# Gathers released in blocks of four buffers, and smaller blocks in the streamed table, in a graph-layer kernel

## The chip, the cores and the metric

The kernel runs on one core of one Trainium2 chip. The metric is the device time of one execution in microseconds. Three timed executions of the kernel before took 1646.1 to 1649.81 us, with a median of 1647.18 us. The profile is one further execution.

## The reference

There are 12,500 nodes with 128 features each, and 200,000 edges that are sorted by their target `dst`. The targets are drawn so that low node numbers have very many edges and high ones few. Every edge has one of four types, and every type has a 128x128 matrix and a bias.

```python
h = jnp.maximum(_layernorm(x, axis=-1), 0.0)
xs = h[src]
for i in range(4):
    msgs = msgs + jnp.where((edge_type == i)[:, None], xs @ W[i] + b[i], 0.0)
out = x + segment_sum(msgs, dst, num_segments=12500)
```

## The kernel before, in words

The edges are cut into 1563 chunks of 128. **Setup** (until about 193 us): `x` is read in spans of three rows a partition (`load_span`, L472), normalized, split into three bf16 parts that add up to the f32 value, and written to a table `htab` in DRAM, 768 bytes a node. The spans lie in the buffers of the pool `rows` (`hpool`, L234), which the gathers take over later. The edges of the first 528 chunks are brought into "slots" (`make_slots`, L797), and the 48 chunks after them are worked from rows of `x` (`add_up_raw`, L610).

**The main part** weaves two independent kinds of work on TensorE.

*Dense work*, for the first 528 chunks, goes in 19 batches. `count` (L938) multiplies one-hot matrices `o` that VectorE makes (L957, L965) into counts of edges for each node, type and source (`pt`, L983), which ScalarE casts to bytes (L989). `multiply` (L1021) then multiplies the whole table by these counts: for each of the 98 blocks `j` of the table, three matmuls with the table as the weights (`pa`, L1033). The table is streamed from DRAM once a batch: SyncE's queue issues one load `hs` (L1029) for `HB` = 6 blocks (L59), 17 loads a batch, into a ring of `STREAM` = 4 buffers (L62). A load waits until TensorE has read the buffer that it fills. Other transfers stand in the same queue in between: the edge lists of later chunks (L210), the finished rows of the output (`out_dram`, L698) and the rows of `x` that are added to the next ones (`xo`, L677).

*Sparse work*, for the other 987 chunks, goes in groups of 16 (60 groups, then 12, 8, 4 and 3). `gather` (L538) is called for the group after the one being worked on. It takes one buffer of `rows` for each two chunks (`HG` = 2) and issues one indirect DMA a chunk from GpSimd's queue: 128 rows of 768 bytes, picked by `srcT`. There are 11 buffers. A gather that fills a buffer waits for the last matmul that reads what lay in it. `sum_up` (L569) multiplies each chunk's rows by a one-hot matrix `oh` (L561), three matmuls a chunk (`ps`, L578); after every four chunks ScalarE copies the sums out (L581). `weigh` (L586) multiplies by the type matrices (`py`, L605), and VectorE adds the result into a ring of output rows (`ring`, L666).

The order on TensorE, VectorE and ScalarE in the main part is written out by the program (`manual_schedule`, L1302): the loop at L1304 takes the steps of `sum_up` for a group, and after each step as many steps of the dense work as `pace` (L1079) says, by columns of matmul. GpSimd's and SyncE's instructions stand in the order that the framework's scheduler gives them. `held_by` (L517) adds a wait to an instruction by hand.

After about 1591 us the dense work is over, and the last groups and output rows follow.

Of the kernel before, what the change touches and what calls it, by code (L numbers as in the profile page):

```python
# [55 lines left out]
C0 = 528  # L56
UB = 27
MANY = 16
HB = 6  # L59
SLOTS = 4  # L60
SETS = 4
STREAM = 4  # L62
# [3 lines left out]
HG = 2  # L66
# [2 lines left out]
SOON = (RAW * 16) + HG  # L69

TURN = 4


@with_exitstack
def kernel(
# [10 lines left out]
    nc = tc.nc  # L86
# [35 lines left out]
    def window_of(c):  # L122

        m = min((c - C0) // G, FULL)
        end = (C0 + (m + 1) * G if m < FULL else T) * P / E
        a_node = E * ((end**2 + 1 / N) ** 0.5 - end)
        return next((n for n in range(8, WIN, 2) if (n - 1) * a_node > P + 5 * P**0.5), WIN)
# [14 lines left out]
    left = threes + len(two)  # L142
# [3 lines left out]
    for i, n in enumerate(sizes_of):  # L146
# [4 lines left out]
        of = alone[3 * many_at : 3 * (many_at + n1)]  # L151
# [69 lines left out]

    srcT = const.tile([P, TURN, P], I32, name="srcT")
    keyT = const.tile([P, TURN, P], F32, name="keyT")
    brow = const.tile([1, BR * BC], I32, name="brow")
# [6 lines left out]
    flag = const.tile([P, 1], I32, name="flag")  # L231

    mid = ExitStack()
    hpool = mid.enter_context(tc.tile_pool(name="rows", bufs=11))  # L234
    opool = mid.enter_context(tc.tile_pool(name="onehots", bufs=2))
    spool = mid.enter_context(tc.tile_pool(name="typed", bufs=2))
    x_ps = mid.enter_context(tc.tile_pool(name="x_ps", bufs=4, space=PSUM))
# [30 lines left out]
    def prep_edges(m0, m1, prep, QB):  # L268
# [16 lines left out]
        for q in range(n):  # L285
            nc.tensor.transpose(pg[:, q, :], sf[:, q, :], ident)
        nc.scalar.copy(srcT[:, m0 % TURN : m0 % TURN + n, :], pg[:, :n, :])
        nc.vector.tensor_copy(head[:, m0:m1], di[:, :n, 0])
# [9 lines left out]
        for q in range(n):  # L298
            nc.tensor.transpose(pk[:, q, :], key[:, q, :], ident)
        nc.scalar.copy(keyT[:, m0 % TURN : m0 % TURN + n, :], pk[:, :n, :])  # L300
        nc.vector.tensor_reduce(ends[:, m0:m1, 0], rel[:, :n], AX.X, ALU.max)
# [4 lines left out]
    def prep_steps(m, prep):  # L306
# [26 lines left out]
        nc.tensor.transpose(pg[:, 1, :], key[:, 0, :], ident)  # L333
        nc.scalar.copy(srcT[:, m % TURN, :], pg[:, 0, :])
        nc.scalar.copy(keyT[:, m % TURN, :], pg[:, 1, :])

# [180 lines left out]
    def held_by(one, by, reason):  # L517
        tc.add_manual_dep(
            one.ins,
            by.name,  # L520
            mybir.DependencyInfo(mybir.DependencyClass.Sync, mybir.DependencyReason.DATA),
            reason=reason,
        )

    def gather_raw(k, by):
# [9 lines left out]
                held_by(one, by, "rows of x come while the table is made, spread over its blocks")  # L535
        return hm

    def gather(t0, g):  # L538
        got = []
        for h0 in range(0, g, HG):  # L540
            hm = hpool.tile([P, HG * D3], BF16, name="hm")
            for i in range(h0, min(h0 + HG, g)):
                at = (t0 + i) % (TURN * P)
                one = nc.gpsimd.indirect_dma_start(  # L544
                    out=hm[:, (i - h0) * D3 : (i - h0 + 1) * D3],
                    out_offset=None,
                    in_=htab,
                    in_offset=bass.IndirectOffsetOnAxis(ap=srcf[:, at : at + 1], axis=0),
                )
                if i == h0 and gates and t0 + i >= SOON:  # L550
                    held_by(one, gates.pop(0), "the first rows come while the slots are made, not ahead of them")
            got.append(hm)
        return lambda i, c: got[i // HG][:, (i % HG * 3 + c) * D : (i % HG * 3 + c + 1) * D]

    def one_hots_of(t0, g):
        K = NT * window_of(C0 + t0)
        oh = opool.tile([P, G, KM], BF16, name="oh")[:, :, :K]

        def make(i):
            at = (t0 + i) % (TURN * P)  # L560
            nc.vector.tensor_scalar(oh[:, i, :], iota_b[:, :K], keyf[:, at : at + 1], None, ALU.is_equal)  # L561

        return oh, [lambda i=i: make(i) for i in range(g)]
# [5 lines left out]
    def sum_up(t0, g, rows, oh, last):  # L569
        win = window_of(C0 + t0)  # L570
        K = NT * win
        sb = spool.tile([P, G * KM], F32, name="sb")[:, : G * K].rearrange("p (g t n) -> p g t n", g=G, t=NT)
        for i0 in range(0, g, SG):
            i1 = min(i0 + SG, g)
            ps = s_ps.tile([P, 512], F32, name="ps")[:, : SG * K].rearrange("p (i n) -> p i n", i=SG)
            for i in range(i0, i1):
                for c in range(3):
                    nc.tensor.matmul(ps[:, i - i0, :], rows(i, c), oh[:, i, :], start=(c == 0), stop=(c == 2))  # L578
                if i % HG and i + 1 < i1:
                    yield (i + 1) / g  # L580
            nc.scalar.copy(sb[:, i0:i1].rearrange("p g t n -> p g (t n)"), ps[:, : i1 - i0, :])  # L581
            yield i1 / g

        finish.append(weigh(t0, g, oh, sb, last))

    def weigh(t0, g, oh, sb, last):  # L586
        win = window_of(C0 + t0)

        def bank():
            to = x_ps.tile([P, G * WIN], F32, name="pt") if last else y_ps.tile([P, G * WIN], F32, name="py")  # L590
            return to[:, : G * win].rearrange("p (g n) -> p g n", g=G)

        ohv = oh.rearrange("p g (t n) -> p g t n", t=NT)
        pc = bank()
        for t in range(NT):
            nc.tensor.matmul(  # L596
                pc[t * CG : (t + 1) * CG, :g, :], three, ohv[:, :g, t, :], start=True, stop=True, tile_position=(0, t * CG)
            )
        cnt = spool.tile([P, G * WIN], BF16, name="cnt")[:, : G * win].rearrange("p (g n) -> p g n", g=G)
        nc.scalar.copy(cnt[:, :g], pc[:, :g])  # L600
        yield True
        py = bank()
        nc.tensor.matmul(py[:, :g, :], b128, cnt[:, :g, :], start=True, stop=False)
        for t in range(NT):
            nc.tensor.matmul(py[:, :g, :], wsb[:, t, :], sb[:, :g, t, :], start=False, stop=(t == NT - 1))  # L605
        adds.extend(ring_adds(t0, g, lambda i: py[:, i, :], win))
        yield True
# [413 lines left out]
    def multiply(vs, counts):  # L1021
# [3 lines left out]
        pa = a_ps.tile([P, 512], F32, name="pa")  # L1025
        for j0 in range(0, NW, HB):
            j1 = min(j0 + HB, NW)
            hs = hsp.tile([P, HB, D3], BF16, name="hs")
            nc.sync.dma_start(hs[:, : j1 - j0, :], htab.rearrange("(p j) f -> p j f", j=NW)[:, j0:j1, :])  # L1029
# [265 lines left out]
    leaving = []  # L1295
    soon = []
    rows = gather(RAW * G, G)
    oh, made = one_hots_of(RAW * G, G)
    for m in made:
# [4 lines left out]
    for gi, (t0, g) in list(enumerate(zip(starts, sizes)))[RAW:]:  # L1304
# [12 lines left out]
        if gi < final:  # L1317
            rows = gather(starts[gi + 1], sizes[gi + 1])
        parts = -(-g // HG)
        when = min(2, parts - 1)  # L1320
        todo = len(side) + G + 1 + (G if finish else 0)
        for j, part in enumerate(sum_up(t0, g, *now, gi >= FULL)):
            late, tails[:] = list(tails), []
            while work and spent < pace(gi, part):
                spent = next(work, None)
                if spent is None:
                    work = None
            for f in late:
                f()
            if checks and next(checks[0], None) is None:  # L1330
                checks.pop(0)
            if j == 0:
                if finish:
                    next(finish[0])
                if gi < final:
                    oh, made = one_hots_of(starts[gi + 1], sizes[gi + 1])
                    side += made
            if j == when:
                if finish:
                    next(finish.pop(0))  # L1340
                side.append(lambda: [ending.pop(0)() for _ in list(ending)])
                side += adds
                adds.clear()
                todo = min(todo, len(side) * parts // max(1, parts - 1 - j))
            left = todo * (parts - 1 - j) // parts - (0 if j >= when else todo - len(side))
            while side and len(side) > left:
                side.pop(0)()
            for _ in range(2):
                if leaving:
                    leaving.pop(0)()  # L1350
# [171 lines left out]
```

## Time and profile before

| | us |
|---|---|
| median of three executions | 1647.18 |
| lowest, highest | 1646.1, 1649.81 |
| the profiled execution's own time | 1651.06 |
| its span, first to last instruction | 1649.2 |
| TensorE's mean granted clock | 0.957 of full speed |
| dense and sparse work together on TensorE | 193 to 1591 |

A group of instructions is named by source line, engine and operation, with the tiles written and read (`pa<-counts,hs`), its count, its busy time, the mean of one in ns, and the engine's idle time just before them with what ended it. "issue" is idle time that ended by nothing that the profile shows; "remote" a wait whose releaser is not told. PEld is the load of weights into TensorE, and a q behind an engine's name stands for its queue of instructions (SPq issues DMAs). The chain of waits follows the work that ended last back to the start.

### The profile page before, as it was taken

The page shows a single profiled execution, that of the slowest core. Times are in us where ns is not written, and L with a number is a line of the kernel's source. Part 1 is how long each engine was busy: PE and PEld are TensorE (multiplying, and loading weights), DVE is VectorE, ACT ScalarE, POOL GpSimd, SP SyncE. Part 2 cuts the span into 40 slices and gives each one's busy share as a digit, 9 for nine tenths or more (in the row PEclk, how much of TensorE's full clock was granted, in tenths as well). Part 3 has the DMA queues.
Part 4 walks back from the last instruction along what each step waited for, and adds up shares of the span by engine and source line. Part 5 has one row for each costly group of instructions (what it writes and reads, how often), then busy time and mean ns, then how long its engine had stood idle before and what let it go on. Part 6 is the DMA issues. An engine that isn't in the chain of part 4 may idle for free.

```text
span 1649.2 us, 33169 instructions
## 1 busy us (share of the span) xinstructions
PE 1457.4 (88%) x11293; PEld 958.5 (58%) x11293; DVE 1041.5 (63%) x5387; ACT 458.7 (28%) x1121; POOL 1011.6 (61%) x1062
## 2 busy tenths in 40 slices
PE   5678789999899999999999999999999999998975
PEld 2236476666566566666666666656565656565654
DVE  8792977666585766657576666657564756574333
ACT  6494222222222222222222222222222222222011
POOL 7435566666666666666666666666666566666562
PEclk9785799999999999999999999999999999999997
DMA  7452377766667766666666667666666566666652
GB/s 221 129 212 75 107 220 220 217 197 213 200 206 211 217 194 212 197 208 208 207 202 201 200 209 220 181 210 203 180 219 198 175 194 211 184 189 193 210 169 70
DMA packets 138411, 317.02 MB, mean 192 GB/s; under 512 B 25880, under 2 KB 78666, under 8 KB 138235
## 3 DMA queue, kind: packets, MB, share of 16 engines
q1 hardware_dynamic: 89323, 214.61, 41.7%
q0 software_dynamic: 48912, 100.24, 20.8%
q8 instruction: 89, 1.46, 0.4%
q14 instruction: 87, 0.71, 0.1%
HBM read 298.71 MB, written 16.04 MB: 191 GB/s over the span
## 4 chain that ended last, share of the span: by engine, by line
PE 81%; issue 8%; DVE 8%; ACT 2%; DMA 1%; DVEq 0%; SPq 0%; POOL 0%; ACTq 0%
PE pa L1033 47%; PE pt L983 12%; PE py L605 7%; PE ps L578 7%; DVE o L957 1%; PE pt L1047 1%; PE ps L635 1%; PE py L596 1%; PE pt L691 1%; DVE oh L561 1%; DVE o L965 1%; DVE ring L666 1%; PE pt L857 1%; DVE stt L440 1%; PE pt L854 0%
## 5 line engine op out<-in xcount | busy, mean ns | idle before, releaser
L544 POOL DMA_INDIRECT hm<-htab,srcT x987 | 954.7, 967 | 575.6 <-issue 226.0
L1033 PE MATMUL pa<-counts,hs 128*128 128x324 fp8e4 (+1 forms) x5586 | 1000.5, 304 | 50.2 <-issue 47.1
L1033 PEld LDWEIGHTS <-hs 128*128 128x128 bf16 x5586 | 519.0, 96 | 325.1 <-issue 84.7
L957 DVE TENSOR_SCALAR o<-iota_n,hkT 128x392 bf16<-128x392 f16 x1211 | 401.2, 331 | 75.4 <-PE pt L983 30.6
L983 PE MATMUL pt<-o,o 128*128 128x396 bf16 x1211 | 378.4, 336 | 37.0 <-DVE o L965 20.0
L989 ACT CAST counts<-pt 128x396 int32<-128x396 f32 x506 | 242.1, 493 | 500.5 <-PE pt L983 172.1
L561 DVE TENSOR_SCALAR oh<-iota_b,keyT 128x56 bf16<-128x56 bf16 (+8 forms) x987 | 167.7, 261 | 265.6 <-PE ps L578 94.6
L581 ACT COPY sb<-ps 128x224 f32<-128x224 f32 (+8 forms) x247 | 98.4, 399 | 480.3 <-PE pt L983 165.0
L578 PE MATMUL ps<-oh,hm 128*128 128x56 bf16 (+8 forms) x2961 | 189.1, 198 | 38.0 <-issue 35.3
L578 PEld LDWEIGHTS <-hm 128*128 128x128 bf16 x2961 | 163.0, 99 | 96.5 <-issue 49.1
L666 DVE TENSOR_TENSOR ring<-ring,py 128x14 f32 (+7 forms) x960 | 167.7, 175 | 65.0 <-PE pa L1033 13.0
L965 DVE TENSOR_SCALAR o<-iota,loT 128x128 bf16<-128x128 bf16 x660 | 178.4, 270 | 0.0
L983 PEld LDWEIGHTS <-o 128*128 128x128 bf16 x1211 | 114.8, 97 | 96.2 <-DVE o L965 27.4
L965 DVE TENSOR_SCALAR o<-iota,loT,byT 128x128 bf16<-128x128 bf16 x461 | 155.4, 337 | 0.0
L605 PE MATMUL py<-sb,wsb 128*128 128x224 f32 (+7 forms) x480 | 129.5, 412 | 1.3 <-issue 1.0
L605 PEld LDWEIGHTS py<-sb,wsb 128*128 128x128 f32 x480 | 88.2, 196 | 27.6 <-issue 5.6
L997 DVE COPY bi<-counts 128x27 int32<-128x27 int32 (+1 forms) x19 | 4.2, 220 | 113.3 <-issue 64.7
L528 POOL DMA_INDIRECT hx<-in_x_dram,srcT x48 | 51.3, 1069 | 35.9 <-DVE stt L440 22.4
L600 ACT CAST cnt<-py 128x224 bf16<-128x224 f32 (+7 forms) x60 | 23.7, 396 | 93.3 <-PE ps L578 29.9
L461 ACT ACTIVATE h<-hm,nmrt,rstdt 128x128 f32<-128x128 f32 x98 | 43.0, 493 | 1.0 <-DVE mvt L444 0.5
L1047 PE MATMUL pt<-sd,wsb 128*128 128x81 f32 (+1 forms) x152 | 25.8, 325 | 4.6 <-issue 4.6
L490 PE MATMUL ps<-h,ident 128*128 128x384 f32 (+1 forms) x34 | 16.3, 563 | 12.7 <-issue 11.6
(235 smaller groups left out, 666.6 us busy)
## 6 DMA issues: line engine op xcount, KB each, us to landing
hs<-htab SPq DMA_DIRECT2D x304, 576.0 KB
hm<-htab,srcT POOLq DMA_INDIRECT x987
htab<-h SPq DMA_DIRECT2D x32, 288.0 KB
xo<-in_x_dram SPq DMA_DIRECT2D x24, 256.0 KB
out_dram<-xo SPq DMA_DIRECT2D x24, 256.0 KB
hs<-htab SPq DMA_DIRECT2D x19, 192.0 KB
hm<-in_x_dram SPq DMA_DIRECT2D x18, 192.0 KB
hm<-in_x_dram SPq DMA_DIRECT2D x14, 168.0 KB
```

Source lines behind the costliest of these rows:

```text
L528: one = nc.gpsimd.indirect_dma_start(out=hm[:, i * D : (i + 1) * D], out_offset=None, in_=x, in_offset=bass.IndirectOffsetOnAxis(ap=srcf[: ...
L544: one = nc.gpsimd.indirect_dma_start(out=hm[:, (i - h0) * D3 : (i - h0 + 1) * D3], out_offset=None, in_=htab, in_offset=bass.IndirectOffse ...
L561: nc.vector.tensor_scalar(oh[:, i, :], iota_b[:, :K], keyf[:, at : at + 1], None, ALU.is_equal)
L578: nc.tensor.matmul(ps[:, i - i0, :], rows(i, c), oh[:, i, :], start=(c == 0), stop=(c == 2))
L581: nc.scalar.copy(sb[:, i0:i1].rearrange("p g t n -> p g (t n)"), ps[:, : i1 - i0, :])
L605: nc.tensor.matmul(py[:, :g, :], wsb[:, t, :], sb[:, :g, t, :], start=False, stop=(t == NT - 1))
L666: nc.vector.tensor_tensor(to, to, of(i), ALU.add)
L957: one = nc.vector.tensor_scalar(o2[:, k, :NB], iota_n, hkT[:, s : s + 1], None, ALU.is_equal)
L965: one = nc.vector.tensor_scalar(o1[:, k], iota_1, loT[:, s : s + 1], by, ALU.is_equal, ALU.mult)
L983: one = nc.tensor.matmul(pb, o1, o2, start=first, stop=last)
L989: nc.scalar.copy(counts[:, :, i * NT : (i + 1) * NT], pb.rearrange("p (b t) -> p b t", t=NT))
L1033: nc.tensor.matmul(pa[:, : 3 * nu * NT].rearrange("p (m v) -> p m v", m=3), hs[:, j - j0, c * D : (c + 1) * D], of, start=(j == 0 and c == 0),
```

## The change

Three things are changed. The ring of row buffers has 12 instead of 11 places. A load of the streamed table carries 5 blocks instead of 6, so there are 20 loads a batch (19 of five blocks and one of three), and the four buffers of the ring hold 20 blocks instead of 24. And gathers are put into blocks of up to eight chunks, that is four buffers, counted from the start of each group: every gather of a block is made to wait for the matmul that reads the last of the four buffers' earlier contents. `taken` counts buffers, `read` lists the last reading matmul of each buffer in order, and `left` is the number of the reader to wait for; where that matmul is not yet written out when the gather is, `waiting` keeps the gather until it is.

```diff
-HB = 6
+HB = 5
...
+ROWS = 12
+BLOCK = 8
...
-    hpool = mid.enter_context(tc.tile_pool(name="rows", bufs=11))
+    hpool = mid.enter_context(tc.tile_pool(name="rows", bufs=ROWS))
...
+    taken = [0]
+    read = []
+    waiting = {}
...
         for h0 in range(0, g, HG):
+            taken[0] += 1
+            left = taken[0] + (min(h0 // BLOCK * BLOCK + BLOCK, g) - h0 - 1) // HG - 1 - ROWS
             hm = hpool.tile([P, HG * D3], BF16, name="hm")
...
+                if left >= 0:
+                    if left < len(read):
+                        held_by(one, read[left], "a block of rows comes when all of its buffers are free")
+                    else:
+                        waiting.setdefault(left, []).append(one)
...
-                    nc.tensor.matmul(ps[:, i - i0, :], rows(i, c), oh[:, i, :], start=(c == 0), stop=(c == 2))
+                    one = nc.tensor.matmul(ps[:, i - i0, :], rows(i, c), oh[:, i, :], start=(c == 0), stop=(c == 2))
+                if i % HG == HG - 1 or i == g - 1:
+                    for later_one in waiting.pop(len(read), []):
+                        held_by(later_one, one.ins, "a block of rows comes when all of its buffers are free")
+                    read.append(one.ins)
```

## The prediction

> **What bounds the kernel now.** I read the page first: the busy shares, the slices, the chain of waits and the costliest groups.
>
> ```profile
> span 1649.2 us, 33169 instructions
> PE 1457.4 (88%) x11293; PEld 958.5 (58%) x11293; DVE 1041.5 (63%) x5387; ACT 458.7 (28%) x1121; POOL 1011.6 (61%) x1062
> ...
> PE   5678789999899999999999999999999999998975
> ...
> PE 81%; issue 8%; DVE 8%; ACT 2%; DMA 1%; DVEq 0%; SPq 0%; POOL 0%; ACTq 0%
> ...
> L544 POOL DMA_INDIRECT hm<-htab,srcT x987 | 954.7, 967 | 575.6 <-issue 226.0
> L1033 PE MATMUL pa<-counts,hs 128*128 128x324 fp8e4 (+1 forms) x5586 | 1000.5, 304 | 50.2 <-issue 47.1
> ...
> L578 PE MATMUL ps<-oh,hm 128*128 128x56 bf16 (+8 forms) x2961 | 189.1, 198 | 38.0 <-issue 35.3
> ```
>
> TensorE is busy 88% of the span, and it makes 81% of the chain; transfers make 1% of it and GpSimd nothing. The change touches only transfers and the waits ahead of them, so I then asked for the main part alone, in a view by stretches (length, busy time and count of each engine, granted clock, share of the DMA engines, GB/s):
>
> ```profile
> 193.00:1591.00 1398.00, 1290.28 (x10479) 860.47 (x10477) 877.23 (x4608) 336.36 (x805) 888.43 (x918) 0.99 0.66 202
> ```
>
> Here TensorE is busy 1290.3 of 1398.0 us, 92%. All its idle time is 108 us, and that is the most that any better supply could give back. The question is who ends it. Next I grouped the instructions by shape, for the readers of the two kinds of transfer:
>
> ```profile
> L1033 PEld LDWEIGHTS <-hs 128*128 128x128 bf16 x5586 | 519.0, 96 | 325.1 <-issue 84.7
> L578 PEld LDWEIGHTS <-hm 128*128 128x128 bf16 x2961 | 163.0, 99 | 96.5 <-issue 49.1 <-DMA hm<-htab,srcT 3.7
> L983 PEld LDWEIGHTS <-o 128*128 128x128 bf16 x1211 | 114.8, 97 | 96.2 <-DVE o L965 27.4 <-issue 24.1
> ```
>
> Gathers ended 3.7 us of waits in the whole run. No wait is put down to the streamed table; hidden waits for it would stand under "issue". But idle time of that name stands before every kind of matmul: 49.1 us at L578 and 24.1 us at L983, which don't read the stream. So I take it as TensorE's own, and the kernel as bound by TensorE's work.
>
> **Part 1, gathers in blocks.** The same 987 gathers are issued in the same order; only their release moves. How far ahead they run follows from the first and last instruction of each kind in the view of the tile `hm`, and how fast they can go from the timeline:
>
> ```profile
> L578 PE MATMUL ps<-oh,hm x2961: 179/197/294, 154.1 to 1637.0; 128*128 128x56 bf16 x29, 128*128 128x80 bf16 x29, 128*128 128x64 bf16 x26, 128*128 128x88 bf16 x26
> ```
>
> ```profile
> 802.32 0.95 POOL L544 DMA_INDIRECT hm<-htab,srcT  x1 [0.30 <-issue]
> ...
> 803.57 0.94 POOL L544 DMA_INDIRECT hm<-htab,srcT  x1 [0.30 <-issue]
> ...
> 804.81 0.94 POOL L544 DMA_INDIRECT hm<-htab,srcT  x1 [0.30 <-issue]
> ...
> 807.12 0.94 POOL L544 DMA_INDIRECT hm<-htab,srcT  x1 [1.36 <-remote]
> ```
>
> TensorE reads 987 chunks in 1637.0 - 154.1 = 1482.9 us: one in 1.50 us. GpSimd issues one in 0.95 + 0.30 = 1.25 us when it need not wait. So gathers are already close to continuous: a block of eight takes 10.0 us to issue and 12.0 us to read, and bunching is only a pause of some 2 us every 12 us in place of one of some 0.5 us every 3 us.
>
> Before, buffer k waits for the reader of k - 11. After, the buffers k to k + 3 of a block all wait for the reader of k - 9: two buffers later for the first, one for the second, the same for the third, one earlier for the fourth. The twelfth buffer pays for most of the block wait. The first gather of a block is released when two whole blocks, 16 chunks, are still to be read: 24 us. If it lands some 4 us after its release (an estimate: 1.25 us of issue, and 98 KB at even a fifth of the 202 GB/s above, 2.4 us), it has 20 us to spare. The eighth is issued 8.8 us later and read 10.5 us later. What is queued behind the waiting gather on GpSimd is only more gathers, needed later still. **Cost on TensorE: 0**, hidden under 20 us of sparse and dense work; if that cover were gone, each block (some 124 of them) would cost up to the 10 us of its issue. Near the end, the last block waits for buffer 481 where its last gather waited for 482 before, so the tail loses nothing.
>
> GpSimd itself waits less. In the view of waits:
>
> ```profile
> POOL hm L544 <- PE ps L578: 118.7, 85, 4.9
> POOL hm L544 <- PE pt L983: 77.5, 68, 1.5
> POOL hm L544 <- remote: 65.8, 52, 1.7
> POOL hm L544 <- PE pa L1033: 34.9, 30, 1.7
> ```
>
> That is 296.9 us in 235 waits, 1.26 us each; with one wait a block it is at most some 124. But this engine is 0% of the chain, so what it saves is worth 0.
>
> **Part 2, five blocks a load.** Each load shrinks from 576 to 480 KB, and there are 19 x 20 = 380 instead of 323. What SyncE's queue does with its time:
>
> ```profile
> SPq L1029 <- PE ps L578: 352.8, 87, 11.0
> SPq L1029 <- PE pt L983: 272.0, 74, 9.8
> SPq L1029 <- remote: 235.8, 53, 8.3
> SPq L1029 <- PE pa L1033: 212.0, 60, 12.2
> ```
>
> ```profile
> L1033 PE MATMUL pa<-counts,hs x5586: 266/304/479, 193.2 to 1590.9; 128*128 128x324 fp8e4 x189, 128*128 128x240 fp8e4 x11
> L1029 SPq DMA_DIRECT2D hs<-htab x323: 319/320/1877, 115.7 to 1581.3; - x162
> ```
>
> 1072.6 us of the queue's time are waits of these loads for TensorE to free a buffer: the stream is held by its buffers, not by the DMA engines. 57 more issues of 0.32 us, 18 us, fall into those waits: 0. But the lead shrinks. TensorE uses 19 x 98 = 1862 blocks in 1397.7 us, one in 0.75 us. From the release of a buffer to its next use lie three other buffers: 18 blocks or 13.5 us before, 15 blocks or 11.3 us after. The worst place is where the queue stands still for an output row and the rows of `x` for the next one:
>
> ```profile
> 1201.15 10.69 SPq L1029 DMA_DIRECT2D hs<-htab  x2
> 1212.76 0.39 SPq L698 DMA_DIRECT2D out_dram<-xo  x1
> 1217.43 0.38 SPq L677 DMA_DIRECT2D xo<-in_x_dram  x1
> 1218.21 13.73 SPq L1029 DMA_DIRECT2D hs<-htab  x5
> ```
>
> From the store to the next load no table load is issued for 5.45 us. How long a load takes is bounded from both sides: at the start of the stream four of them run nearly alone, and the average rate of the main part was 202 GB/s.
>
> ```profile
> 118.00:120.00 2.00, 1.96 (x10) 1.96 (x10) 2.00 (x16) 2.00 (x6) 1.39 (x3) 0.50 1.00 406
> ```
>
> 576 KB take 1.5 us at 406 GB/s and 2.9 us at 202; 480 KB take 1.2 to 2.4. So at such a place a buffer has 13.5 - 5.45 - 2.9 = 5.1 us to spare at the least before and 11.3 - 5.45 - 2.4 = 3.4 us after, at the average pace. Where matmuls on the table come without a break the pace is faster: 15 of them took 2.31 us (row below, in part 3), so a block takes about 0.43 us, 15 blocks 6.5 us, and nothing is left: 6.5 - 5.45 - 1.2 to 2.4 is -0.2 to -1.4 us. The page's list of DMA issues counts the loads, and the view of waits tells how long stores stand:
>
> ```profile
> hs<-htab SPq DMA_DIRECT2D x304, 576.0 KB
> ...
> xo<-in_x_dram SPq DMA_DIRECT2D x24, 256.0 KB
> ```
>
> ```profile
> SPq L698 <- DVE xo L696: 38.3, 14, 8.5
> ```
>
> Of the 24 fetches some 20 fall into the main part, each with such a pause. Lower end: 0. Upper end: 20 x 1.4 = 28 us. TensorE rarely keeps the fast pace for 15 blocks, since a group of chunks comes in between, so I stay near the low end: one or two of the 20 pauses run dry for about a microsecond, **+2 us**. In the built program one table load stands between store and fetch at about half of these places, which helps.
>
> **Part 3, order and signals.** In the built program the order on TensorE, VectorE and ScalarE from the first group on is the same; in the setup some instructions change places, because the spans of `x` find a twelfth buffer. The setup's chain goes through TensorE, VectorE and ScalarE work that is all still there: 0, with 2 us either way for the range. One thing goes away: a reader has to signal GpSimd only at the end of a block. Of each four chunks the second's signal went to GpSimd alone (the fourth's also to ScalarE), so some 245 matmuls no longer signal. Whether a signal costs TensorE time, the timeline shows for the table's matmuls, of which every 18th signals:
>
> ```profile
> 1579.15 2.31 PE L1033 MATMUL pa<-counts,hs 128*128 128x324 fp8e4 x15
> ...
> 1583.96 1.88 PE L1033 MATMUL pa<-counts,hs 128*128 128x324 fp8e4 x12
> ```
>
> 15 take 2.31 us and 12 take 1.88 us: 0.143 us for each one more, and no step in between. I take 0. The far end is that all of L578's idle time under "issue" came from its signals, and half of them go: 17.6 us saved.
>
> The Trainium skill, "TensorE: Matmul & The Clock Gate", section "The cost: per-tile semaphore tail", says that increments on completion serialize, about 26.3 ns each; by that the 245 signals would be worth 6.4 us, an estimate from that page. The two rows above don't show such a step, and recorded ends of matmuls are modelled, so the rows can't rule it out.
>
> **The sum.** 0 (gathers) + 2 (stream) + 0 (order, signals) = +2 us. Against the profiled execution, 1649.2 us of span and 1651.06 us in all, that is 1653 us; it lies 3.9 us above the median of the three executions, so against the median it is 1647.2 + 2 = **1649 us**.
>
> **Rivals.**
> *The stream runs dry* (slower). The lead of 15 blocks is too short at each of the 20 pauses on SyncE's queue. For it: the 5.45 us without a load, and that a store has waited as long as 8.5 us. Against it: no wait on the stream shows now. It decides where 15 blocks take less than the pause and the load, 5.45 + 2.4 = 7.9 us. At half of the upper end, 14 us, the time is 1661 us.
> *Fewer signals* (faster). TensorE pays for each signal in a way that its records hide. For it: "issue" before L578. Against it: the even spacing above. Some 6 us, between 0 and 17.6: 1641 us.
> *Bunching moves VectorE* (faster or slower). VectorE's one-hots run beside GpSimd's issues, and pauses of 2 us instead of 0.5 change which are beside which. For it: VectorE is 8% of the chain, and 27.4 us of weight loads wait for `o`. Against it: the sum of GpSimd's busy time stays. A tenth of 27.4 is 3 us, either way; it is inside the forecast's own range.
> *It does not bunch.* Since a block takes 10 of 12 us to issue, the change hardly does what it says; that is my forecast's reason, and gives the same time.
>
> **How the numbers follow.** About 0.2%, 3.3 us, is what a measurement of this kernel can tell from no change: faster is below 1643.9, slower above 1650.5. Forecast 0.46, own range 1645 to 1653, of which 0.40 is within 0.2% and 0.06 above; the dry stream 0.30; fewer signals 0.24. So faster 0.24, same 0.40, slower 0.36. The range takes in the middle of both rivals: 1639 to 1661.
>
> **What would show it.** Right: GpSimd's waits on TensorE number about a third, with 1.25 us between gathers in a block; L1029 x380; the idle time before L1033 and L578 within a few us of before. A dry stream shows as idle time before L1033 that grows by 10 us or more, just after a store. Costly signals show as less "issue" before L578. I am wrong in the main if TensorE's busy time itself moves by more than 5 us.

## The result, and the profile after

The changed kernel took a median of 1924.45 us (1915.99 to 1928.17, four executions) against 1646.64 us (1646.04 to 1649.81, four executions) of the kernel before in the same job: a ratio of 1.1668, 95% interval 1.1646 to 1.169. It is 278 us slower, where the forecast was 2 us.

The page of the changed kernel first (its lines are shifted: gathers L552, selecting matmuls L591, the table's matmuls L1050, its loads L1046):

```profile
span 1914.3 us, 32924 instructions
PE 1563.9 (82%) x11293; PEld 986.0 (52%) x11293; DVE 1033.5 (54%) x5387; ACT 462.4 (24%) x1121; POOL 1004.0 (52%) x1062
...
PE   4776878888888888888888888888888788888874
...
PEclk9776899998999999899999999988999998989996
...
L552 POOL DMA_INDIRECT hm<-htab,srcT x987 | 948.7, 961 | 844.2 <-PE ps L591 459.7
L1050 PE MATMUL pa<-counts,hs 128*128 128x324 fp8e4 (+1 forms) x5586 | 1075.8, 314 | 165.8 <-issue 155.2
...
L591 PE MATMUL ps<-oh,hm 128*128 128x56 bf16 (+8 forms) x2961 | 197.8, 202 | 59.2 <-issue 41.3
```

The counts of work are the same. TensorE's slices read 8 where they read 9, all along the main part, so this is no pause in one place. Its idle time before the table's matmuls grew from 50.2 to 165.8 us, and 155.2 us of that is "issue": nothing that the profile shows was waited for. The same stretch as before, in the view by stretches:

```profile
193.00:1861.00 1668.00, 1409.13 (x10542) 896.98 (x10543) 879.38 (x4663) 342.10 (x809) 889.22 (x926) 0.94 0.57 171
```

The main part takes 1668.0 us instead of 1398.0. TensorE is idle for 1668.0 - 1409.1 = 258.9 us (107.7 before), and busy for 118.8 us more with the same instructions, much of it because the granted clock is 0.94 instead of 0.99 (6% of 1668 us is 100 us, 1% of 1398 is 14, so some 86 us by this estimate). So the loss of 270 us is some 151 us of new idle time and 119 us of slower work.

Neither transfer is late. With the packets of the trace matched to the gathers and loads in order of time, a gather has landed at least 7.7 us ahead of its first reader (9.2 before), and a full table load at least 1.9 us ahead (2.0 before). The waits of GpSimd and ScalarE:

```profile
POOL hm L552 <- PE ps L591: 459.7, 99, 11.8
```

```profile
ACT sb L598 <- remote: 369.7, 72, 11.4
```

GpSimd waits rarely and long, as the change asks. But ScalarE, too, now waits up to 11.4 us for something that the profile can't name, though the multiplications it copies from were long done.

### The profile page after: what moved, and what is told of

The parts are those of the page before. It is cut to its first block, busy times and chain, and to the rows that moved or that the text cites. A ratio compares the mean times of both kernels' runs of the same rounds, so it can differ in the third digit from the quotient of the medians.

```text
span 1914.3 us, 32924 instructions
## 1 busy us (share of the span) xinstructions
PE 1563.9 (82%) x11293; PEld 986.0 (52%) x11293; DVE 1033.5 (54%) x5387; ACT 462.4 (24%) x1121; POOL 1004.0 (52%) x1062
## 5 line engine op out<-in xcount | busy, mean ns | idle before, releaser
L552 POOL DMA_INDIRECT hm<-htab,srcT x987 | 948.7, 961 | 844.2 <-PE ps L591 459.7
L1050 PE MATMUL pa<-counts,hs 128*128 128x324 fp8e4 (+1 forms) x5586 | 1075.8, 314 | 165.8 <-issue 155.2
L1050 PEld LDWEIGHTS <-hs 128*128 128x128 bf16 x5586 | 531.3, 99 | 490.9 <-issue 249.3
L974 DVE TENSOR_SCALAR o<-iota_n,hkT 128x392 bf16<-128x392 f16 x1211 | 394.2, 325 | 184.6 <-remote 74.1
L1000 PE MATMUL pt<-o,o 128*128 128x396 bf16 x1211 | 397.8, 352 | 60.4 <-issue 32.7
L591 PE MATMUL ps<-oh,hm 128*128 128x56 bf16 (+8 forms) x2961 | 197.8, 202 | 59.2 <-issue 41.3
L591 PEld LDWEIGHTS <-hm 128*128 128x128 bf16 x2961 | 170.4, 101 | 125.5 <-issue 75.7
L622 PE MATMUL py<-sb,wsb 128*128 128x224 f32 (+7 forms) x480 | 137.5, 434 | 3.3 <-issue 3.3
L622 PEld LDWEIGHTS py<-sb,wsb 128*128 128x128 f32 x480 | 95.2, 211 | 31.6 <-issue 8.6
L652 PE MATMUL ps<-ohf,hx 128*128 128x40 f32 x96 | 21.5, 412 | 5.1 <-ACT hx L463 2.5
```

Source lines behind the costliest of these rows:

```text
L552: one = nc.gpsimd.indirect_dma_start(out=hm[:, (i - h0) * D3 : (i - h0 + 1) * D3], out_offset=None, in_=htab, in_offset=bass.IndirectOffse ...
L591: one = nc.tensor.matmul(ps[:, i - i0, :], rows(i, c), oh[:, i, :], start=(c == 0), stop=(c == 2))
L974: one = nc.vector.tensor_scalar(o2[:, k, :NB], iota_n, hkT[:, s : s + 1], None, ALU.is_equal)
L1000: one = nc.tensor.matmul(pb, o1, o2, start=first, stop=last)
L1050: nc.tensor.matmul(pa[:, : 3 * nu * NT].rearrange("p (m v) -> p m v", m=3), hs[:, j - j0, c * D : (c + 1) * D], of, start=(j == 0 and c == 0),
```

## What happens inside one block

One block of eight gathers, from its first gather at 808.93 us, in the view by stretches (the columns are length, then busy time and count of TensorE, its weight loads, VectorE, ScalarE and GpSimd, then clock, DMA share, GB/s):

```profile
808.90:811.80 2.90, 2.90 (x27) 1.92 (x25) 2.73 (x15) 1.15 (x3) 2.26 (x3) 1.00 0.24 48
811.80:814.60 2.80, 2.80 (x26) 1.87 (x24) 1.28 (x8) 0.49 (x1) 2.19 (x3) 1.00 0.88 281
814.60:817.40 2.80, 2.27 (x21) 1.32 (x18) 1.79 (x10) 0.00 (x0) 2.19 (x3) 1.00 0.53 151
817.40:820.30 2.90, 1.06 (x4) 0.25 (x4) 0.00 (x0) 0.37 (x1) 1.09 (x2) 1.00 0.27 71
820.30:821.20 0.90, 0.85 (x11) 0.66 (x12) 0.59 (x3) 0.76 (x2) 0.00 (x0) 1.00 0.00 0
```

While GpSimd issues, the others run dry one after the other: ScalarE, then VectorE, then TensorE, which does 4 matmuls in 2.9 us. Then all start together. The timeline of the end of it:

```profile
817.48 0.12 PEld L1050 LDWEIGHTS <-hs 128*128 128x128 bf16 x2 [0.98 <-issue]
817.49 0.31 PE L1050 MATMUL pa<-counts,hs 128*128 128x324 fp8e4 x1 [0.62 <-issue]
817.85 0.95 POOL L552 DMA_INDIRECT hm<-htab,srcT  x1 [0.30 <-issue]
818.20 0.30 PE L1050 MATMUL pa<-counts,hs 128*128 128x324 fp8e4 x1 [0.40 <-issue]
818.91 0.13 PEld L1050 LDWEIGHTS <-hs 128*128 128x128 bf16 x2 [1.30 <-issue]
818.92 0.37 ACT L598 COPY sb<-ps 128x256 f32<-128x256 f32 x1 [5.20 <-remote]
818.94 0.45 PE L1050 MATMUL pa<-counts,hs 128*128 128x324 fp8e4 x2 [0.43 <-issue]
820.33 0.12 PEld L1050 LDWEIGHTS <-hs 128*128 128x128 bf16 x2 [1.29 <-issue]
820.35 0.45 PE L1050 MATMUL pa<-counts,hs 128*128 128x324 fp8e4 x2 [0.96 <-issue]
820.37 0.32 SPq L1046 DMA_DIRECT2D hs<-htab  x1
```

Matmuls start at 817.49, 818.20, 818.94 and 820.35 us, in steps of about 0.71 us or twice that, where 0.14 us is normal; the first waits only for a table load that landed at 808.30 us, the other three carry no wait at all. Below I call this a crawl: time of 0.1 us or more in which TensorE neither multiplies nor loads weights, ahead of an instruction without a wait, pieces under 2 us apart taken as one. SyncE's load and TensorE go on within 0.04 us of each other, at 820.33 to 820.37 us, which is 11.4 us after the block's first gather.

The trace also keeps the times at which a semaphore (the counter by which one engine signals another) was updated. In this block, six matmuls that add to TensorE's semaphore end from 812.67 to 816.70 us; the six updates that follow are recorded at 813.21, 818.90, 820.35, 820.41, 820.58 and 820.63 us. ScalarE's copy starts at 818.92 us, right after the second of them.

That 11.4 us is no accident. I call gathers with less than 0.4 us between them a run, and sorted the crawls of the main part by the run in which they began (the last two rows are an experiment told below):

| profile | gathers in a run | runs | crawls | median end of a crawl, after the run's first gather |
|---|---|---|---|---|
| before | 4 | 179 | 80 | 5.68 us |
| before | 6 | 12 | 10 | 8.51 us |
| after | 8 | 111 | 111, in 109 runs | 11.34 us |
| blocks of two buffers | 4 | 187 | 67 | 5.68 us |
| blocks of two buffers | 8 | 18 | 17 | 11.37 us |

5.68 / 4, 8.51 / 6 and 11.34 / 8 are all 1.42 us. GpSimd issues one gather in 1.25 us; the crawls end as if something behind it took 1.42 us for each, and until it is done with the whole run the other engines get few signals through. The kernel before has the same crawls, only shorter: 69 us of TensorE's time, against 196 us after.

That the signals themselves are late can be counted. These are the matmuls of the main part that add to TensorE's semaphore, and how many of them have an update of it on record within 0.1 us of their end, by whether that end falls into the first 1.42 n us of a run of n gathers (the last three rows are experiments told below):

| profile | inside: prompt, of | outside: prompt, of |
|---|---|---|
| before | 151 of 1331 | 76 of 100 |
| after | 274 of 994 | 266 of 267 |
| before, half the gathers | 381 of 545 | 884 of 884 |
| after, half the gathers | 287 of 706 | 555 of 555 |
| block wait alone, chip 11 | 1258 of 1281 | 13 of 13 |

(Ends of matmuls are modelled, and some updates are not on record: 1413 are there of 1556 in the profile after.) In the first four, signals are late mostly while gathers are under way, and once the changed kernel's runs are through, all but one are prompt. On the chip of the last row they are hardly ever late.

## The experiments

The theories. **A**: the wait for a whole block harms by itself (a long wait of GpSimd on TensorE). **B**: the smaller table loads. **C**: the twelfth buffer or the placement that comes with it. **D**: the loss depends on the chip or job. **E**: the gathers themselves hold the other engines' signals, 1.42 us each, and what the change does is to make runs of eight. **F**: crawls come from TensorE or the table's stream. The jobs ran on several chips, which matters below.

### The parts alone

Five blocks a load (`HB = 5`) in the kernel before:

> The kernel before with one edit: the streamed table's buffers hold five blocks each instead of six (11 buffers of rows, each gather waits for its own buffer). Theory A, the wait of whole blocks of gathers costs the 278 us: this run stays within 10 us of before (1637 to 1657 us), pe's idle before L1050 as in before (about 50 us for the multiplications, against 166 us in the changed kernel). Theory B, the smaller loads of the table cost them: 1850 to 1930 us. Theory C, the twelfth buffer of rows or the placement in SBUF that comes with it costs them: within 10 us of before, like A.

The same with 12 buffers:

> The kernel before with two of the three edits: five blocks a buffer of the table and 12 buffers of rows; each gather still waits for its own buffer alone. Theory A (the wait of whole blocks): within 10 us of before (1637 to 1657 us). Theory B (five blocks a load): 1850 to 1930 us. Theory C (the twelfth buffer): 1850 to 1930 us. So A is told from C here, and B from C by the run with five blocks alone.

The block wait with the sizes of before:

```diff
-HB = 5
+HB = 6
-ROWS = 12
+ROWS = 11
```

> The changed kernel with the sizes of before: six blocks a buffer of the table, 11 buffers of rows, and the wait of eight gathers on the last of the four buffers they fill. Theory A (the wait of whole blocks): 1850 us or more, since 11 buffers leave one buffer less ahead than the changed kernel's 12; GpSimd's waits on the selecting multiplications sum to 400 us or more (460 us in the changed kernel, 119 us before). Theory B and theory C: within 10 us of before.

The changed kernel with half the block:

```diff
-BLOCK = 8
+BLOCK = 4
```

> The changed kernel with blocks of four chunks: gathers wait for the last of the two buffers they fill, not of four; five blocks a load and 12 buffers of rows as in the changed kernel. Theory A in the form that the length of GpSimd's wait matters (longest 11.8 us in the changed kernel, 4.9 before): between the two, about 1700 us. Theory A in the form that any wait for a block breaks the flow: 1850 us or more. Theory B and theory C: 1850 to 1930 us, as the changed kernel.

Measured, in this order: 1468.95 us (ratio 1.0005, 0.9995 to 1.0014), 1467.33 us (0.9994, 0.9984 to 1.0003), 1473.41 us (1.0035, 1.0022 to 1.0047) and 1467.91 us (0.9994, 0.9985 to 1.0004). But the kernel before took 1468.4 us in this job, not 1646.6. None of A, B and C foresaw that. On this chip (numbered 11) the block wait costs 5 us, and the page of the block wait alone shows a TensorE that never crawls, and 5.2 us of waits for gathers that land late (this kernel has 11 buffers, not 12):

```profile
PE 1402.2 (95%) x11293; PEld 949.7 (65%) x11293; DVE 1037.7 (70%) x5387; ACT 475.3 (32%) x1121; POOL 1017.9 (69%) x1062
...
L1050 PE MATMUL pa<-counts,hs 128*128 128x324 fp8e4 (+1 forms) x5586 | 981.2, 303 | 0.5 <-ACT sd L1060 0.5
L1050 PEld LDWEIGHTS <-hs 128*128 128x128 bf16 x5586 | 519.5, 96 | 247.0 <-issue 0.7
...
L591 PE MATMUL ps<-oh,hm 128*128 128x56 bf16 (+8 forms) x2961 | 179.3, 197 | 5.8 <-DMA hm<-htab,srcT 5.2
```

"issue" before the table's weight loads is 0.7 us, against 84.7 in the kernel before's profile. A block of eight gathers on this chip, again by stretches:

```profile
805.60:808.50 2.90, 2.90 (x23) 2.29 (x22) 2.90 (x15) 0.49 (x1) 2.26 (x3) 1.00 0.95 354
808.50:811.30 2.80, 2.80 (x30) 1.93 (x29) 2.70 (x21) 1.16 (x3) 2.19 (x3) 1.00 0.37 122
811.30:814.10 2.80, 2.80 (x26) 1.90 (x24) 2.60 (x16) 1.01 (x3) 2.19 (x3) 1.00 0.92 301
814.10:817.00 2.90, 2.90 (x26) 1.93 (x25) 2.16 (x12) 0.57 (x2) 2.09 (x3) 1.00 0.69 206
```

GpSimd issues at the same pace and nobody runs dry. There are 45 runs of sixteen gathers in this profile and not one crawl.

### The changed kernel and the block wait once more

> The changed kernel itself, unchanged, beside the kernel before in the same job. In the first experiments the kernel before took 1468.4 us, not the 1646.6 us of the result, and the block wait alone cost 0.35%. Theory D, the 278 us belong to the way the job of the result ran: where the kernel before takes about 1468 us the changed kernel takes 1466 to 1474 us (ratio 0.998 to 1.004), and only where the kernel before takes about 1647 us does it take about 1924. Theory A (the block wait together with five blocks a load breaks the flow anywhere): over 1600 us beside 1468.

> The block wait alone once more (six blocks a load, 11 buffers of rows). If the kernel before takes about 1468 us in this job: 1473 us again (ratio 1.0035). If it takes about 1647 us: theory A (the wait of whole blocks, on such a job) 1850 us or more; theory B (five blocks a load, on such a job) within 10 us of the kernel before.

This job ran on chip 15, and there the kernel before took 1649.41 us. The changed kernel took 1936.29 us (ratio 1.1738, 1.1709 to 1.1766), the block wait alone 1909.63 us (1.1591, 1.1557 to 1.1626). So the block wait carries 260 of 287 us, B and C together the other 27, if the parts add up. D holds for the block wait, which cost 260 us here and 5 us on chip 11; the changed kernel as a whole was not run on chip 11. The waits of the block wait alone, on this chip:

```profile
POOL hm L552 <- PE ps L591: 377.8, 83, 11.2
```

The same program on chip 11 waited there 49 times, for 77.9 us in all.

### Pauses on GpSimd

To split a block of eight into two runs of four, with the block wait kept, GpSimd clears a scratch tile twice after every fourth gather, and `after_it` (an order without a signal) keeps the clears in place:

```diff
+            if h0 // HG % 2 == 1:
+                for _ in range(2):
+                    rest = nc.gpsimd.memset(pause, 0.0)
+                    after_it(rest, one)
+                paused.append(rest)
```

> The changed kernel, its block wait kept, with a pause of GpSimd (two clears of a scratch tile, about 1.1 us) after every fourth gather, so that a block of eight gathers becomes two runs of four; nothing else is changed. Theory E (run length): in the jobs in which the kernel before takes 1647 to 1649 us, TensorE's crawl ends 1.42 us times the number of gathers in the run after the run begins (5.68 us for four, 11.34 for eight), and begins some 3.4 to 9.5 us after it; runs of four crawl in 80 of 179 cases, runs of eight nearly always. So two runs of four should bring the time from 1930 down to 1640 to 1720 us. Rival A (the wait of GpSimd for a whole block is itself what harms): the wait is the same, so 1880 us or more. In a job in which the kernel before takes about 1468 us: no crawl by either theory, 1468 to 1490 us.

One clear after every second gather, with the block wait, and without it:

```diff
+            rest = nc.gpsimd.memset(pause, 0.0)
+            after_it(rest, one)
+            paused.append(rest)
```

> The changed kernel, its block wait kept, with a pause of GpSimd (one clear, about 0.5 us) after every second gather: runs of two, and a pair every 3.0 us against 2.84 us that a run of two would take at 1.42 us each. Theory E: runs of two crawl in 2 of 35 cases of the kernel before, so hardly any crawl is left; the time is then set by GpSimd, 195 us ahead of the main part, 890 gathers at 1.5 us, some 60 us behind: about 1590 us, which is under the kernel before (1649 us) although GpSimd does more. Rival A: 1880 us or more, unless GpSimd falls so far behind that it no longer waits. In a job in which the kernel before takes 1468 us: 1560 to 1600 us, as GpSimd becomes the bound.

> As the run before it, but without the block wait (the kernel before with five blocks a load, 12 buffers of rows and the pauses). Theory E: the same 1590 us, within 20 us of it, since only the length of the runs counts. Rival A: the kernel before's own 1649 us or more. In a job in which the kernel before takes 1468 us: 1560 to 1600 us.

> The changed kernel with blocks of four gathers in place of eight, no pause. Theory E: runs of four, as most runs of the kernel before (179 of 244), so within 3% of it where it takes 1649 us: 1630 to 1700 us. Rival A in the form that any wait for a block harms: 1800 us or more. In a job in which the kernel before takes 1468 us: 1468 us again.

This job came to chip 11 (before: 1468.36 us), so it says nothing on E: 1633.11, 1569.68, 1563.46 and 1468.17 us (ratios 1.1135, 1.0699, 1.0648 and 1.0006). The first missed its 1468 to 1490 us, because I had left GpSimd's own work out of that number. Its chain of waits and its clears:

```profile
POOL 58%; PE 15%; issue 14%; DVE 7%; DMA 4%; ACT 1%; DVEq 0%; SPq 0%; POOLq 0%; ACTq 0%
...
L580 POOL MEMSET pause<- 128x480 f32 x494 | 258.1, 523 | 14.3
```

GpSimd has become the bound. Two more runs of the same kernels on chip 11 gave 1570.83 and 1468.33 us. Then the next job came to chip 4:

> The changed kernel, its block wait kept, with a clear of about 0.5 us on GpSimd after every second gather. Where the kernel before takes about 1649 us: theory E (the length of a run of gathers decides; a run of two is done after 2.84 us, before TensorE's crawl begins) 1570 to 1600 us, under the kernel before, with hardly any of TensorE's idle time left to issue; rival A (the wait for a whole block of buffers) 1880 us or more. Where it takes 1468 us: 1570 us once more.

> The changed kernel with blocks of four gathers in place of eight, no pause. Where the kernel before takes about 1649 us: theory E, runs of four as in the kernel before, 1630 to 1700 us, crawls that end 5.68 us after a run begins; rival A in the form that any wait for a block harms, 1800 us or more. Where it takes 1468 us: 1468 us once more.

> The changed kernel itself. Where the kernel before takes 1468 us (theory D): 1466 to 1474 us, ratio 0.998 to 1.004, since its parts alone gave 1.0005, 0.9994 and 1.0035 there. Where it takes about 1649 us: 1924 to 1936 us again, ratio about 1.17.

Here the kernel before took 1650.43 us and the changed kernel 1930.57 us (ratio 1.1718, 1.1683 to 1.1754). Blocks of two buffers took 1679.38 us (1.0175, 1.0157 to 1.0194), inside E's range and far from A's 1800: half the block takes away 251 of the 280 us. The table above has the mechanism inside one profile: of its 18 runs of eight 17 crawl, until 11.37 us, and of its 187 runs of four 67, until 5.68 us. Its rows for the table's matmuls and for GpSimd's longest kind of wait:

```profile
L1050 PE MATMUL pa<-counts,hs 128*128 128x324 fp8e4 (+1 forms) x5586 | 1015.7, 307 | 51.3 <-issue 49.1
```

```profile
POOL hm L552 <- PE ps L591: 87.3, 35, 5.3
```

The pauses after each pair brought 1682.67 us (1.0181, 1.0141 to 1.0221): 248 us under the changed kernel with 494 instructions more on GpSimd, far from A's 1880, but not E's 1570 to 1600 either.

```profile
L1066 PE MATMUL pa<-counts,hs 128*128 128x324 fp8e4 (+1 forms) x5586 | 1012.0, 304 | 47.1 <-issue 35.9
...
L998 DVE TENSOR_SCALAR o<-iota,loT 128x128 bf16<-128x128 bf16 x660 | 236.5, 358 | 0.0
```

There are still 88 crawls in 459 runs of two, 64 us in sum. They end 2.96 us after the run begins in the middle case; 41 end at 2.7 to 3.1 us, 12 at 5.7 to 6.0 us and two at 8.8 us, two and three pairs on. A pair takes 2.84 us at 1.42 us a gather, and in half of the cases the next one begins 2.90 us after it or sooner, not the 3.0 us that I had planned. With 0.06 us or less in between, the runs all but join, and I read the misses so that what is held by one pair is not through when the next begins; no run tests that. (VectorE's one-hots also grew, 270 to 358 ns at the line shown, beside GpSimd's clears.)

### Half the gathers

Is it the gathers at all? Every second one is left out, so each buffer gets one, and both chunks are multiplied with its rows:

```diff
-            for i in range(h0, min(h0 + HG, g)):
+            for i in range(h0, h0 + 1):
```

> The kernel before with every second gather left out: each buffer of two chunks gets one gather, and both chunks are multiplied with its rows (so half the rows are not read; TensorE's work and the table's stream stay as they are). Where the kernel before takes about 1649 us: theory E (signals are held while gathers are under way, 1.42 us each) leaves runs of two, 890 x 1.42 = 1264 us under way become 632, and TensorE's unsynchronised idle time falls from 69 us to under 15: 1470 to 1540 us. Rival F (the crawls of the kernel before come from TensorE itself or from the table's stream): 1620 to 1650 us. Where the kernel before takes 1468 us: 1460 to 1470 us.

The kernel before with groups of two chunks in place of four in `sum_up`:

```diff
-SG = 4
+SG = 2
```

> The kernel before with one constant changed: the selecting multiplications come in groups of two chunks in place of four, so a buffer of rows comes free by itself and gathers come in runs of two, without pauses. Where the kernel before takes about 1649 us: theory E by the length of a run, 1560 to 1630 us; theory E by the share of time under way (1264 of 1395 us of the main part), the same 1649 us within 15. Where the kernel before takes 1468 us: 1465 to 1485 us (247 more evictions on ScalarE, which idles).

On chip 15 again, where the kernel before took 1672.56 us in this job. Half the gathers: 1481.36 us (ratio 0.8861, 0.8839 to 0.8882), and no crawl is left:

```profile
L1033 PE MATMUL pa<-counts,hs 128*128 128x324 fp8e4 (+1 forms) x5586 | 980.6, 302 | 0.5 <-ACT sd L1043 0.5
...
L1033 PEld LDWEIGHTS <-hs 128*128 128x128 bf16 x5586 | 519.2, 96 | 247.3 <-issue 0.7
```

F falls. TensorE's "issue" time in the kernel before, and all but some 13 us of the time by which it is slower here than on chip 11 (1468 us), come from the gathers: with half of them TensorE's rows are those of chip 11. The run leaves out a gather's issue and its transfer alike, so it doesn't tell which of the two holds the signals.

Groups of two: 1681.68 us (1.0061, 1.0039 to 1.0084). This run does not tell what it was made for: 181 of its 247 runs still have four gathers, so the runs were not split.

Last, the same cut in the changed kernel, which keeps the block wait:

> The changed kernel with every second gather left out (both chunks of a buffer are multiplied with the rows of the first; half the rows are not read). The block wait, the table's loads and the 12 buffers stay; a block is a run of four gathers. Where the kernel before takes 1649 to 1673 us: theory E, runs of four that end 5.7 us after they begin, some half of about 120 of them with a crawl of 0.4 us, and signals held for 632 us in place of 1264: 1485 to 1540 us, 400 us under the changed kernel, although GpSimd waits for whole blocks as before and longer. Rival A (the wait for a block harms by itself): 260 us over the 1481 us of the kernel before with half its gathers, about 1740 us. Where the kernel before takes 1468 us: 1465 to 1475 us.

On chip 7 (before: 1650.24 us) it took 1491.49 us (0.903, 0.9013 to 0.9046).

```profile
L1050 PE MATMUL pa<-counts,hs 128*128 128x324 fp8e4 (+1 forms) x5586 | 981.2, 302 | 1.2 <-issue 0.7
```

```profile
POOL hm L552 <- PE ps L591: 600.5, 96, 14.6
```

GpSimd waits longer for its blocks than in the changed kernel, 600.5 us and up to 14.6 us at a time, and TensorE does not mind: 2 crawls in 114 runs of four. A is dead. It also shows that the length of a run is not all: runs of four crawl 80 times in 179 where the next run follows within a few us, and 2 times in 114 where GpSimd then rests.

No kernel here beats the kernel before with its full work: the best, five blocks and 12 buffers without the block wait, is at 0.9994 (0.9984 to 1.0003), on chip 11 alone.

## Why the prediction was wrong

- **What bounds the kernel.** The first step that failed is in this part: "idle time of that name stands before every kind of matmul ... So I take it as TensorE's own". It was not TensorE's own. It was the mark that GpSimd's gathers leave on every engine, and with half the gathers it went from 47.1 us to nothing. That it stood before every kind of matmul, also those that read nothing of the stream, was the clue, and I read it the wrong way. On chip 11, where signals are prompt, TensorE is idle for 4.6 of 1231 us in the main part (five blocks a load), against 107.7 of 1398 here.
- **Part 1, gathers in blocks: cost 0.** This is the term that failed. The working on the transfers was right: a gather still lands at least 7.7 us early, and GpSimd issues in 1.25 us. Its waits on TensorE, those by "remote" included, fell from 235 to 116, about half and not the third that I named; but "GpSimd itself waits less" was wrong, for these waits grew from 296.9 to 517.8 us. "What is queued behind the waiting gather on GpSimd is only more gathers" was right too. What was missing is what stands beside a run of gathers: everything that needs a signal. Runs of four became runs of eight, and the time in which signals are held went from 5.68 to 11.34 us at a time. This term was put at 0 and measured 260 us (block wait alone, chip 15). "bunching is only a pause of some 2 us every 12 us in place of one of some 0.5 us every 3 us" says it: I took the pauses as worthless, and they are when the signals get through: 266 of 267 are prompt there, 274 of 994 within the runs.
- **Part 2, five blocks a load: +2 us.** Measured alone on chip 11: 1468.95 against 1468.4 us, nothing to be told from zero. Where the kernel before takes 1649 us it was not run alone; there, the sizes together add 27 us to the block wait (1936.29 against 1909.63). A full load landed 3.4 us after its issue in the middle case (3.5 before), where I had reckoned 1.2 to 2.4, but none lands late, so the rival of the dry stream is not what happened; why the sizes add 27 us is open. The page counts 361 + 19 = 380 loads, as forecast.
- **Part 3, order and signals: 0.** The rival of the fewer signals did not come: 1556 of TensorE's instructions signal instead of 1739, and the time rose. Chip 11 tells it apart: with five blocks a load and 12 buffers, blocks of two buffers take the count from 1797 to 1556, and the time stays, 1467.33 and 1467.91 us. The 6.4 us of the prediction's estimate are not seen there.
- **Bunching moves VectorE** was priced at 3 us either way. VectorE does run dry in the block shown, but through the held signals, as the other engines do.
- The signs that I named did their work: TensorE's busy time moved by 106.5 us where 5 was the limit, and idle time before the table's matmuls by 115.6 us. The second was also my sign of a dry stream, and alone it would have pointed at the wrong cause.
- **The clock.** The forecast had no term for it. TensorE's granted clock in the main part fell from 0.99 to 0.94, some 86 us of the 270 by the estimate above. The Trainium skill, "TensorE: Matmul & The Clock Gate", section "What's actually happening", says that the gate halves the clock after an idle window of about 3.4 us. The trace agrees in the length: 7 stretches at half clock in the main part before, 51 after, 198 us in all, each of them 3.4 or 6.8 us long. But the window need not be idle throughout here: in the 3.4 us ahead of the 51 stretches TensorE was busy for 45% in the middle case, and ahead of 48 of them it had no idle piece longer than 1.22 us.

What stays open: what inside the chip takes 1.42 us a gather and holds the signals, and why chip 11 has none of it. No run here looks there. It is not that rows arrive more slowly: in the block wait alone half of the gathers have landed 2.4 us after their issue on chip 15, and 3.1 us on chip 11. That signals are held is read from the late updates of TensorE's semaphore, counted above, from ScalarE's 5.20 us wait "remote" for sums that were done, and from engines that start within 0.04 us of each other. Every execution on record comes with a recorded span and clock, so no run shows whether the recording itself takes part. Runs of eight with long rests between them, which would part the length of a run from the share of time under way, were not tried.

## What to carry to other kernels

Idle time under "issue" that stands before every kind of an engine's instructions need not be the engine's own: sort it by what another engine was doing when it began and ended, and a fixed multiple (here 1.42 us a gather) gives the culprit away. Gathers issued back to back can cost the engines that don't wait for them, so a release that lets them bunch is not free because the data comes early; short runs with rests between them, or fewer gathers, are what helped here against the changed kernel. And measure such a change on more than one chip before judging it: it cost 17% in three jobs, and its block wait alone 0.35% on another chip.

## What the runs showed of the hardware that was not expected

- The same kernel takes 1468 us on one chip (three jobs) and 1649 to 1673 us on three others (four jobs), with the same TensorE work. No profile from the one has a crawl; the kernel before's profile above has 69 us of them. Its other losses (granted clock, late starts of the other engines) were not measured one by one.
- In the other jobs a run of n gathers (128 rows of 768 bytes each) holds other engines' signals until 1.42 n us after it began, by where the crawls end, for n = 4, 6 and 8 (1.44 n in the job in which the kernel before took 1673 us: 5.76 us for four), while TensorE goes on in steps of 0.71 us in the block shown. After that time 266 of 267 of its signals were prompt, within it 274 of 994.
- A clear of 128x448 f32 on GpSimd took 503 ns, and beside such clears VectorE's 128x128 one-hots took 358 ns instead of 270.
